# All rows of layer 1 turned by VectorE, and another order at the beginning, in a two-layer graph kernel on one Trainium2 core

## The chip, the core and the metric

The kernel runs on one core of one Trainium2 chip. The metric is the device time of one execution in microseconds; the median of several runs counts. TensorE multiplies, VectorE and ScalarE work elementwise, GpSimd takes small steps, and SyncE issues most of the transfers between memory and the on-chip buffer. [...]

## What is computed

4096 rows `x` of 512 numbers and a 4096 x 4096 matrix `adj` go through two layers. Layer 0 is softmax attention inside graphs of 128 rows each, so that one graph is one tile of 128 rows; layer 1 is attention over the nonzero entries of `adj` with 8 heads of 64 numbers.

```python
# layer 0
h = jnp.maximum(_layernorm(x), 0.0)
query, key, value = h @ Wq.T + bq, h @ Wk.T + bk, h @ Wv.T + bv
a = jnp.where(mask, query @ key.T * scale, 0.0)          # mask: same graph
scores = (a + adj + adj) * jnp.where(mask, 1.0, -1000000.0)
x = x + (softmax(scores) * mask) @ value
# layer 1
h = jnp.maximum(_layernorm(x), 0.0)
mx = jnp.einsum('nf,hfd->hnd', h, W)
logits = s_i[:, :, None] + t_j[:, None, :]               # s, t: mx times a_origin, a_dst
attn = softmax(where(adj > 0, logits, -inf))
x = x + concat over heads of attn @ mx
```

In layer 1 the term `s_i` cancels in the softmax. So each tile j of rows gives a `part`: exp(t_j) times its projected rows, and exp(t_j) itself. Then each of the 32 tiles of output is a product of the 0/1 mask of `adj` with all 32 parts, and a division.

## The kernel before

It runs in three stages. First `fold` turns the weights of query and key and multiplies them, so that one matrix M serves for both. Then layer 0 goes through 16 pairs of tiles; beside it, all of `adj` is read once, its mask packed into bytes and written to `a_d`, and the first tiles of layer 1 are projected. A second loop projects the other tiles of layer 1. The third stage is the aggregation, 32 times 96 matmuls.

A projection needs the rows of layer 1 turned (features on the partitions). There are two ways in the kernel: `relu_T` has TensorE turn the tile by four transposes; `turn` and `move` have VectorE turn it in 32x32 blocks, four tiles together, and bring the blocks to their places by a write to `hT_d` and a read of it. Before the change tiles 0 to 15 go the first way, 16 to 31 the second (`MIXED` = 16). NT is 32 tiles, KC 4 pieces of 128 features, BY 4, B 32, G 2.

```python
    def relu_T(ps_pool, hn, dst):

        pt = ps_pool.tile([P, KC, P], F32, name="pt")
        for k in range(KC):
            nc.tensor.transpose(pt[:, k, :], hn[:, ts(k, P)], ident)
        nc.scalar.activation(dst, pt, AF.Relu)
# ... (cut)
    def fold(sb, tmp, work, ps_t, ps_p, loads, first):
# ... (cut)
        wkT_sb = load_weight(tmp, wkT, "wkT_sb", KC, tag="lo")
        wqT_sb = load_weight(tmp, wqT, "wqT_sb", KC, tag="lo")
        loads()
# ... (cut)
        nat = []
        for n, wT in enumerate((wkT_sb, wqT_sb)):
            w = tmp.tile([P, KC, D], F32, name=f"w{n}", tag="lo")
            for k in range(KC):
                pt = ps_t.tile([P, KC, P], F32, name="pt")
                for m in range(KC):
                    nc.tensor.transpose(pt[:, m, :], wT[:, k, ts(m, P)], ident)
                nc.scalar.copy(w[:, :, ts(k, P)], pt)
                if n == 0 and k == 0:
                    rows = [spread_bias(b) for b in (bk_sb, bq_sb)]
            nat.append(w)
        wk, wq = nat
# ... (cut) u_col, c_sb: VectorE; then M = wq . wk on TensorE, u_col spread at m == 2
# ... (cut)
    def project1(ps_m, hT, w1x):

        pm = [ps_m.tile([P, D], F32, name="pp") for _ in range(2)]
        for g, n in ((1, HW + H), (0, HW)):
            for k in range(KC):
                nc.tensor.matmul(
                    pm[g][:, :n], hT[:, k, :], w1x[:, k, g * HW : g * HW + n],
                    start=(k == 0), stop=(k == KC - 1),
                )
        return pm
# ... (cut)
            def begin1():
                row = sb2.tile([P, D], F32, name="row1")
                nc.sync.dma_start(row, x1_d[len(rows1)])
                norm(row, row)
                rows1.append(row)

            def turned1(row):
                hT = sb2.tile([P, KC, P], F32, name="hT1")
                relu_T(ps_t, row, hT)
                return hT
# ... (cut)
            def prepare(i, hT, part):
                pm = project1(ps_p, hT, w1x)
                finish(weights(i, pm), pm, part)
# ... (cut)
                def attend(sT, v, g, t):
                    i = G * g + t
                    po = ps_p.tile([P, D], F32, name="pp")
                    nc.tensor.matmul(po, sT[:, t, :], v, start=True, stop=True)
                    x1 = sb.tile([P, D], F32, name="x1")
                    nc.vector.scalar_tensor_tensor(
                        x1, po, rs_all[:, i : i + 1], xg[g][:, t, :], ALU.mult, ALU.add
                    )
                    nc.scalar.dma_start(x1_d[i], x1)
# ... (cut)
                for g in range(NG):   # 16 pairs of tiles
# ... (cut) load_pair(g + 2); at g == 1: w1x = load_w1(pool1, sb)
                    s = scores(g, hT, gT, r, *look)
                    prepare_on(last)
                    if last:
                        begin1()
                    if not last:
                        ngT = queries(nhT)
                    sT = turned(s)
                    prepare_on(3 <= g and g % 2)

                    for _ in range({2: 1, NG - 2: 1, NG - 1: 0}.get(g, int(3 <= g and g % 2))):
                        begin1()
                    nvs = []
                    for t in range(G):
                        look_on(t)
                        if not last and t == 0:
                            nvs.append(values(nhT, t))
                        attend(sT, vs[t], g, t)
                        prepare_on(last and t == 0)
                        if not last and t:
                            nvs.append(values(nhT, t))
                    if not last:
                        hT, r, gT, vs, look = nhT, nr, ngT, nvs, nlook
                    if g + 2 < NG:
                        nhT, hns = turned0(g + 2)
                        nr = row_terms(hns)
# ... (cut) the second loop: VectorE, ScalarE, GpSimd and SyncE in written order
            def turn(i):
                c, b = divmod(i, BY)
                if b == 0:
                    blocks[c] = sb4.tile([P, P // B, KC, BY, B], F32, name="blocks")
                nc.vector.transpose(
                    blocks[c][:, :, :, b], rows[i].rearrange("p (k q f) -> p q k f", k=KC, f=B)
                )
                if b == BY - 1:
                    nc.sync.dma_start(hT_d[c], blocks[c].rearrange("p q k b r -> p q (k b r)"))

            def move(c):
                hT = sb5.tile([P, P // B, KC, P], F32, name="hT4")
                for q in range(P // B):
                    nc.sync.dma_start(
                        hT[ts(q, B)].rearrange("p u k m -> p u (k m)"),
                        hT_d[c, :, q].rearrange("(u f) w -> f u w", f=B),
                    )
                for u in range(BY):
                    hTs[c * BY + u] = hT[:, u]
# ... (cut)
                for i in range(n, NT):
                    far, near = i + AHEAD, i + 2
                    if near + 1 < MIXED:
                        load(near + 1)
                    load(far + 2)
                    if far % BY == 1 and MIXED + BY < far <= NT + 1:
                        move(far // BY - 1)
# ... (cut) from far == NT + 1 on: the mask of the first tile of the aggregation
                    low()
                    if far < NT:
                        of[far] = moments(rows[far])
                    if near < MIXED:
                        of[near] = moments(rows[near])
                    if MIXED < far <= NT:
                        turn(far - 1)
                    if i + 1 < MIXED:
                        hTs[i + 1] = sb2.tile([P, KC, P], F32, name="hT1")
                        relu_T(ps_t, rows[i + 1], hTs[i + 1])
                    pm = project1(ps_p, hTs[i], w1x)
                    if before:
                        low = finish(*before, later=True)
                    if near < MIXED:
                        norm(rows[near], rows[near], of[near])
                    if far < NT:
                        norm(rows[far], rows[far], of[far])
                    e = weights(i, pm)
                    halves = (1, 0)
                    if i < MIXED:
                        halves = (0,)
                        for h in range(H // 2, H):
                            nc.scalar.mul(
                                e[:, ts(h, HD)], pm[1][:, ts(h - H // 2, HD)],
                                e[:, ES + h : ES + h + 1],
                            )
                    before = (e, pm, part_tile(lo if i < LO else hi, i), halves)
                    if far < NT:
                        nc.scalar.activation(rows[far], rows[far], AF.Relu)
```

Pools hold the tiles: `bufs` is the number of buffers of one name, and a new tile waits until the oldest of its name has been read.

## Time and profile before

| what | value |
|---|---|
| device time, median of 3 | 938.12 us (937.1 to 938.38) |
| span of the profiled run | 936.6 us, 13145 instructions |
| beginning, up to the first `wv` product | 0 to 29.2 us |
| layer 0, 16 pairs | from there to about 355 us |
| second loop, projections of layer 1 | to about 443 us |
| aggregation | to the end |
| mean DMA rate over the span | 167 GB/s, 156.63 MB |
| `adj` loads | 64 of 1024 KB, median 12.2 us from issue to landing |

The page's groups give for each line of the kernel the engine, the operation, the tiles that it writes and reads, the shapes, the count, then busy time and mean duration of one. Matmuls are pipelined, so the distance between two starts and the duration of one differ. A wait is put down to what released it last. [...]

### The profile page before, as it was taken

What the parts mean: (1) busy time and instruction counts of PE and PEld (TensorE: products, weight loads), DVE (VectorE), ACT (ScalarE), POOL (GpSimd) and SP (SyncE); (2) the same over time, 40 slices, a digit from 0 to 9 for tenths busy, and PEclk for the clock granted to TensorE, in tenths of its full rate; (3) what the DMA queues carried; (4) which work ended last, traced back from release to release, by engine and by line L of the source; (5) the groups of instructions that cost most, each with busy time, mean ns of one, the idle gap of its engine ahead of it and who ended that gap; (6) DMA issues with size and microseconds to landing.
All of it is one profiled execution on the core that took longest, in us unless ns stands there. A gap on an engine that the chain in (4) does not pass through costs nothing.

```text
span 936.6 us, 13145 instructions
## 1 busy us (share of the span) xinstructions
PE 925.9 (99%) x4987; PEld 809.1 (86%) x4987; DVE 462.2 (49%) x992; ACT 268.1 (29%) x539; POOL 180.4 (19%) x344
## 2 busy tenths in 40 slices
PE   8999999999999999999999999999999999999997
PEld 5676677767677778888999999999999999999997
DVE  4678878777775447754463324242424233332412
ACT  4876576667672216532000000000000000000000
POOL 1311212331221116654101010110101010101010
PEclk9999999999999999999999999999999999999999
DMA  9999997989997114764123131312121222313111
GB/s 334 415 382 401 349 351 302 360 344 371 356 354 273 35 35 146 203 200 103 53 61 91 46 90 46 90 51 85 52 85 54 82 71 65 88 48 90 46 45 37
DMA packets 61062, 156.63 MB, mean 167 GB/s; under 512 B 6722, under 2 KB 23490, under 8 KB 52290
## 3 DMA queue, kind: packets, MB, share of 16 engines
q1 hardware_dynamic: 51058, 138.70, 42.9%
q10 hardware_dynamic: 9936, 17.05, 4.9%
q8 instruction: 40, 0.66, 0.3%
q14 instruction: 28, 0.23, 0.1%
HBM read 117.97 MB, written 37.75 MB: 166 GB/s over the span
## 4 chain that ended last, share of the span: by engine, by line
PE 94%; DMA 3%; ACT 2%; DVE 0%; SPq 0%; issue 0%; ACTq 0%
PE pg L315 51%; PE pp L264 12%; PE pp L461 11%; PE pp L473 11%; PE pp L546 3%; PE pss L519 3%; DMA a<-adj 2%; PE pt L136 2%; ACT junk L496 1%; PE pl L315 1%; DMA bv_sb<-bv 1%; PE pss L538 0%; ACT m_sb L239 0%; ACT gT L465 0%; DVE x L548 0%
## 5 line engine op out<-in xcount | busy, mean ns | idle before, releaser
L315 PE MATMUL pg<-part,ata 128*128 128x348 f32 (+1 forms) x1536 | 246.7, 321 | 0.0
L315 PEld LDWEIGHTS pg<-part,ata 128*128 128x128 f32 x1536 | 244.5, 188 | 0.1
L315 PE MATMUL pg<-part,atb 128*128 128x348 f32 x1472 | 236.4, 321 | 0.0
L315 PEld LDWEIGHTS pg<-part,atb 128*128 128x128 f32 x1472 | 234.2, 188 | 0.1
L329 ACT COPY tot<-pg 128x522 f32<-128x522 f32 x31 | 18.6, 600 | 453.4 <-PE pg L315 453.4
L496 ACT ACTIVATE junk<-a 128x2048 bf16<-128x2048 f32 (+15 forms) x92 | 124.5, 1353 | 36.3 <-DMA a<-adj 15.1
L264 PE MATMUL pp<-w1x,hT 128*128 128x256 f32 (+1 forms) x512 | 114.9, 383 | 0.5 <-DVE e L273 0.5
L473 PE MATMUL pp<-wv,hT 128*128 128x512 f32 x256 | 115.0, 593 | 0.3 <-ACT hT L137 0.3
L461 PE MATMUL pp<-hT,m_sb 128*128 128x256 f32 x512 | 113.2, 379 | 0.0
L301 DVE CAST atb<-at 128x4096 fp32r<-128x4096 fp8e4 x16 | 36.7, 2293 | 152.2 <-PE pg L315 152.2
L264 PEld LDWEIGHTS pp<-w1x,hT 128*128 128x128 f32 x512 | 96.0, 190 | 15.0 <-issue 0.9
L461 PEld LDWEIGHTS pp<-hT,m_sb 128*128 128x128 f32 x512 | 96.1, 190 | 12.9 <-issue 0.5
L301 DVE CAST ata<-at 128x4096 fp32r<-128x4096 fp8e4 (+1 forms) x17 | 36.8, 2167 | 140.4 <-PE pg L315 140.3
L146 DVE TENSOR_SCALAR a<-a 128x512 fp8e4<-128x512 f32 x256 | 96.8, 457 | 5.7 <-DMA a_d<-a 5.7
L473 PEld LDWEIGHTS pp<-wv,hT 128*128 128x128 f32 x256 | 47.8, 190 | 54.9 <-issue 53.1
L767 POOL COPY den_all<-tot 128x1 f32<-128x1 f32 x31 | 5.8, 186 | 365.0 <-DVE tot L330 365.0
L771 POOL TENSOR_TENSOR tot<-tot,row 128x512 f32<-128x512 f32 x31 | 39.9, 1288 | 62.2 <-DVE tot L335 58.1
L248 POOL TENSOR_TENSOR part<-e,part 128x522 fp32r<-128x522 f32 x32 | 41.1, 1285 | 12.9 <-ACT part L245 12.7
L122 POOL TENSOR_SCALAR ve<-mv 128x1 f32<-128x1 f32 x64 | 16.3, 259 | 131.1 <-DVE mv L120 131.0
L137 ACT ACTIVATE hT<-pt 128x512 f32<-128x512 f32 x48 | 26.9, 596 | 50.8 <-PE pt L136 40.5
L477 DVE TENSOR_TENSOR v<-pp,bv_sb 128x512 f32<-128x512 f32 x32 | 22.0, 687 | 39.2 <-PE pp L473 39.2
L292 DVE STREAM_TRANSPOSE at<-mw 128x1024 f32<-128x1024 f32 x32 | 39.6, 1238 | 2.1 <-DMA mw<-a_d 2.1
(113 smaller groups left out, 698.4 us busy)
## 6 DMA issues: line engine op xcount, KB each, us to landing
a<-adj SPq DMA_DIRECT2D x64, 1024.0 KB, 12.2
a_d<-a SPq DMA_DIRECT2D x32, 512.0 KB, 10.3
mw<-a_d SPq DMA_DIRECT2D x128, 128.0 KB, 3.9
row<-x_d SPq DMA_DIRECT2D x41, 256.0 KB, 3.5
xg<-x SPq DMA_DIRECT2D x16, 512.0 KB, 5.1
x_d<-x ACTq DMA_DIRECT2D x32, 256.0 KB, 4.3
out<-tot ACTq DMA_DIRECT2D x31, 256.0 KB, 3.7
rowm<-x_d SPq DMA_DIRECT2D x16, 256.0 KB, 5.2
```

Of the source, the lines that this page charges most:

```text
L146: nc.vector.tensor_scalar(a8v[:, u], av[:, u], 0.0, None, ALU.is_gt, saturate=False)
L248: nc.gpsimd.tensor_sub(dst[:, :, 1, :], e3, dst[:, :, 0, :].bitcast(F32))
L264: nc.tensor.matmul(pm[g][:, :n], hT[:, k, :], w1x[:, k, g * HW : g * HW + n], start=(k == 0), stop=(k == KC - 1),)
L292: nc.vector.transpose(at8.rearrange("p c n b -> p (c n b)").bitcast(F32).rearrange("p (c u n) -> p c u n", c=NW, n=B), mw.rearrange("p u ( ...
L301: nc.vector.tensor_copy(at[:, c0 * BY : c1 * BY].rearrange("p (c b) q -> p c b q", b=BY), at8[:, c0:c1].rearrange("p c q b -> p c b q"),)
L315: nc.tensor.matmul(pg[:, : 2 * CW1].rearrange("p (s w) -> p s w", s=2)[:, :, :n], at[:, j, :], part(j)[:, c, :, :n], start=(j == 0), stop= ...
L461: nc.tensor.matmul(pp[:, : G * P], m_sb[:, k, ts(m, P)], hT[:, k, :], start=(k == 0), stop=(k == KC - 1),)
L473: nc.tensor.matmul(pp, hT[:, k, ts(t, P)], wv[:, k, :], start=(k == 0), stop=(k == KC - 1))
L496: nc.scalar.activation(junk[:, c0:c1], a[:, c0:c1], AF.Exp, scale=2.0 * NEG, accum_out=sums[:, n : n + 1],)
L519: nc.tensor.matmul(pss[:, t, :], gT[:, k, ts(t, P)], hT[:, k, ts(t, P)], start=(k == 0), stop=(k == KC - 1),)
L546: nc.tensor.matmul(po, sT[:, t, :], v, start=True, stop=True)
L771: nc.gpsimd.tensor_add(num, num, row)
```

## The change

Tiles 0 to 15 of layer 1 lose their transposes on TensorE. They are normed, put through ReLU by ScalarE, turned by VectorE and moved through DRAM inside layer 0, one row tile in each pair of layer 0 from pair 1 on and two in the last (`fetch`, `begin`, `move`); eight are projected within layer 0 (`prepare`), at pairs 6, 8, 10, 12, 13 and three times in the last. The second loop has one way for all tiles, prepared `AHEAD` = 9 tiles before their use. Buffers make room for it: `gT`, `s` and `sT` have one instead of two, `diag` two instead of three, and `x1` is written over `xg`. TensorE's instructions of layer 0 stand in written order.

At the beginning, `bk` and `bq` are loaded by SyncE behind `wkT`, the broadcast of `bv` by SyncE behind `wvT`; ten transposes of the identity are put ahead of TensorE's work, and the products that spread the biases come after all of `wkT`'s transposes. The sums for `w1x` (`dots`) are spread over pairs 2 to 5. The byte order of the mask follows the new order of the tiles. Code that runs only for inputs outside the fast way is adapted; it isn't run here.

The diff, cut to its core:

```diff
-MIXED = NT // 2
-AHEAD = 8
+AHEAD = 9
+WARM = 10
# ... (cut)
-    nc.scalar.dma_start(bq_sb, bq)
     bk_sb = const.tile([P, KC], F32, name="bk_sb")
-    nc.scalar.dma_start(bk_sb, bk)
# ... (cut)
-        order = ("p (c b u q) -> p u c b q", "p (c u b q) -> p u c b q")[h]
-        av = a.rearrange(order, c=NW // 2, b=BY, q=B)
+        av = a.rearrange("p (c u b q) -> p u c b q", c=NW // 2, b=BY, q=B)
# ... (cut)
+        nc.sync.dma_start(bk_sb, bk)
+        nc.sync.dma_start(bq_sb, bq)
# ... (cut)
+        pt = ps_t.tile([P, KC, P], F32, name="pt")
+        for _ in range(WARM):
+            nc.tensor.transpose(pt[:, 0, :], ident, ident)
# ... (cut)
-                if n == 0 and k == 0:
+                if n == 0 and k == KC - 1:
# ... (cut)
-            rows1 = []
-
-            def begin1():
-                row = sb2.tile([P, D], F32, name="row1")
-                nc.sync.dma_start(row, x1_d[len(rows1)])
-                norm(row, row)
-                rows1.append(row)
-
-            def turned1(row):
-                hT = sb2.tile([P, KC, P], F32, name="hT1")
-                relu_T(ps_t, row, hT)
-                return hT
+            keep = prep.enter_context(
+                tc.tile_pool(name="keep", bufs=1, side="right", reuse_waits="tile")
+            )
+            blocks, hTs = {}, {}
+
+            def turn(i, row, pool):
+
+                c, b = divmod(i, BY)
+                if b == 0:
+                    blocks[c] = pool.tile([P, P // B, KC, BY, B], F32, name="blocks")
+                nc.vector.transpose(
+                    blocks[c][:, :, :, b], row.rearrange("p (k q f) -> p q k f", k=KC, f=B)
+                )
+                if b == BY - 1:
+                    nc.sync.dma_start(hT_d[c], blocks[c].rearrange("p q k b r -> p q (k b r)"))
+
+            def move(c):
+
+                hT = keep.tile([P, P // B, KC, P], F32, name="hT4", bufs=2)
+                for q in range(P // B):
+                    nc.sync.dma_start(
+                        hT[ts(q, B)].rearrange("p u k m -> p u (k m)"),
+                        hT_d[c, :, q].rearrange("(u f) w -> f u w", f=B),
+                    )
+                for u in range(BY):
+                    hTs[c * BY + u] = hT[:, u]
+
+            rows = {}
+
+            def fetch(i):
+                rows[i] = sb2.tile([P, D], F32, name="row1", bufs=1)
+                nc.sync.dma_start(rows[i], x1_d[i])
+
+            def begin(i):
+                norm(rows[i], rows[i])
+                nc.scalar.activation(rows[i], rows[i], AF.Relu)
+                turn(i, rows[i], keep)
+                if i + 1 < 2 * LO:
+                    fetch(i + 1)
# ... (cut)
-                    gT = sb.tile([P, KC, G * P], F32, name="gT")
+                    gT = sb.tile([P, KC, G * P], F32, name="gT", bufs=1)
-                        sb.tile([P, G, P], F32, name="diag", bufs=3),
+                        sb.tile([P, G, P], F32, name="diag"),
-                    s = sb.tile([P, G, P], F32, name="s")
+                    s = sb.tile([P, G, P], F32, name="s", bufs=1)
-                    sT = sb.tile([P, G, P], F32, name="sT")
+                    sT = sb.tile([P, G, P], F32, name="sT", bufs=1)
-                    x1 = sb.tile([P, D], F32, name="x1")
+                    x1 = xg[g][:, t, :]
                     nc.vector.scalar_tensor_tensor(
-                        x1, po, rs_all[:, i : i + 1], xg[g][:, t, :], ALU.mult, ALU.add
+                        x1, po, rs_all[:, i : i + 1], x1, ALU.mult, ALU.add
# ... (cut)
-                    nc.scalar.dma_start(bv_sb, bv.to_broadcast([P, D]))
+                    nc.sync.dma_start(bv_sb, bv.to_broadcast([P, D]))
# ... (cut)
+                with tc.manual_schedule(engines={mybir.EngineType.PE}):
+                    for g in range(NG):
+                        last = g + 1 == NG
+                        if g == 1:
+                            w1x, dots = load_w1(pool1, sb2, tag="e")
+                        if 2 <= g < 2 + KC:
+                            dots(g - 2)
+                        nlook = seen()
+
+                        def look_on(t):
+                            if not last:
+                                i = G * (g + 1) + t
+                                nlook[2].append(read(i, nlook[0][:, t, :], nlook[1][t]))
+
+                        s = scores(g, hT, gT, r, *look)
+                        if last:
+                            prepare()
+                        else:
+                            ngT = queries(nhT)
+                        sT = turned(s)
+                        if g in (6, 8, 10, 12, 13, NG - 1):
+                            prepare()
+
+                        if g == 1:
+                            fetch(0)
+                        for i in (NG - 2, NG - 1) if last else (g - 1,) if g > 1 else ():
+                            begin(i)
+                        if g > BY and g % BY == 1:
+                            move(g // BY - 1)
+                        if g + 2 < NG:
+                            load_pair(g + 2)
+                        nvs = []
+                        for t in range(G):
+                            look_on(t)
+                            if not last and t == 0:
+                                nvs.append(values(nhT, t))
+                            attend(sT, vs[t], g, t)
+                            if last and t == 0:
+                                prepare()
+                            if not last and t:
+                                nvs.append(values(nhT, t))
+                        if g == 1:
+                            begin(0)
# ... (cut)
+            upper = {j: part_tile(hi, j) for j in range(LO, NT)}
+                first = LO + AHEAD
+                for i in range(first - 1, first + 2):
+                    load(i)
+                move(LO // BY + 1)
+                norm(rows[first - 1], rows[first - 1])
+                nc.scalar.activation(rows[first - 1], rows[first - 1], AF.Relu)
                 before = None
+                for i in range(LO, NT):
+                    far = i + AHEAD
                     load(far + 2)
-                    if far % BY == 1 and MIXED + BY < far <= NT + 1:
+                    if far % BY == 1 and LO + AHEAD < far <= NT + 1:
# ... (cut)
-                    if near < MIXED:
-                        of[near] = moments(rows[near])
-                    if MIXED < far <= NT:
-                        turn(far - 1)
-                    if i + 1 < MIXED:
-                        hTs[i + 1] = sb2.tile([P, KC, P], F32, name="hT1")
-                        relu_T(ps_t, rows[i + 1], hTs[i + 1])
+                    if far <= NT:
+                        turn(far - 1, rows[far - 1], (keep, sb4)[(far - 1) // BY % 2])
# ... (cut)
-                    e = weights(i, pm)
-                    halves = (1, 0)
-                    if i < MIXED:
-                        halves = (0,)
-                        for h in range(H // 2, H):
-                            nc.scalar.mul(
-                                e[:, ts(h, HD)], pm[1][:, ts(h - H // 2, HD)],
-                                e[:, ES + h : ES + h + 1],
-                            )
-                    before = (e, pm, part_tile(lo if i < LO else hi, i), halves)
+                    before = (weights(i, pm), pm, upper[i])
```

## The prediction

> **What bounds the kernel now.** I read the page first, then the waits of TensorE before the aggregation, then TensorE's timeline at the seams, and last the waits of the DMA queue. The page:
>
> ```profile
> PE 925.9 (99%) x4987; PEld 809.1 (86%) x4987; DVE 462.2 (49%) x992; ACT 268.1 (29%) x539; POOL 180.4 (19%) x344
> PE 94%; DMA 3%; ACT 2%; DVE 0%; SPq 0%; issue 0%; ACTq 0%
> ```
>
> TensorE is busy 925.9 of 936.6 us and carries 94% of the chain that ended last. Busy does not mean at its peak, so I asked for TensorE's own waits in the first 445 us (columns: who waited for whom, us in total, times, longest):
>
> ```profile
> PE pt L198 <- DMA wkT_sb<-wkT: 3.9, 1, 3.9
> PE pp L264 <- DVE e L273: 0.5, 1, 0.5
> PE pp L236 <- ACT m_sb L239: 0.3, 1, 0.3
> PE pp L473 <- ACT hT L137: 0.3, 1, 0.3
> ```
>
> That is all: 3.9 us before the first weight arrives and 1.1 us later. One more 0.4 us hides behind pipelined ends: the chain between 197 and 212 us runs through an adjacency load, ScalarE's reads and `sT` (L540). So nothing that only shortens a wait of another engine can help. What helps is an instruction taken off TensorE, or TensorE's useful work beginning earlier. The timeline of TensorE shows the cost of what the change removes (columns: start us, us with pipelined end, line, operation, tiles, count):
>
> ```profile
> 358.95 0.60 PE L136 MATMUL pt<-ident,rown 128*128 128x128 f32 x4
> 359.39 3.67 PE L264 MATMUL pp<-w1x,hT 128*128 128x264 f32 x16
> 362.90 0.60 PE L136 MATMUL pt<-ident,rown 128*128 128x128 f32 x4
> 363.33 3.67 PE L264 MATMUL pp<-w1x,hT 128*128 128x264 f32 x16
> ```
>
> The starts count, not the durations: from the first transpose to the first matmul of the projection it is 359.39 - 358.95 = 0.44 us, from there to the next tile's transposes 3.51. So one tile's four transposes take some 0.435 us, 109 ns each, though each is listed with 272 ns, and a projection takes 3.51. Further on, ten projections without transposes go from 379.12 to 414.86 with one wait of 0.5: again 3.52 each.
>
> The beginning, again TensorE's timeline:
>
> ```profile
> 3.92 1.08 PE L198 MATMUL pt<-ident,wkT_sb 128*128 128x128 f32 x4 [3.92 <-DMA wkT_sb<-wkT]
> 4.80 1.91 PE L184 MATMUL pp<-ident,bk_sb 128*128 128x128 f32 x8
> 6.51 1.91 PE L184 MATMUL pp<-ident,bq_sb 128*128 128x128 f32 x8
> 8.21 2.00 PE L198 MATMUL pt<-ident,wkT_sb 128*128 128x128 f32 x12
> 10.12 2.63 PE L198 MATMUL pt<-ident,wqT_sb 128*128 128x128 f32 x16
> 12.59 0.59 PE L236 MATMUL pp<-w,w 128*128 128x512 f32 x1
> ```
>
> Sixteen bias matmuls take 3.41 us, 213 ns each; the sixteen transposes of `wqT` take 2.47 with small gaps. The array is slow at first, and the loads are slow too. The first piece of `wkT` lands 2.9 us after its issue and the others 7.1 after theirs, at about 9 us: with them goes the broadcast of `bv` on ScalarE's queue, which the chain shows from 1.74 for 6.89 us. The last of `wqT`, issued at 4.8 with some 7.2 to landing, is there at 12.0, and the product of the two weights starts at 12.59. Loads end this stage.
>
> [...]
>
> **The change, part by part.**
>
> 1. *Transposes off TensorE.* Before, tiles 0 to 15 of layer 1 are turned by TensorE: 36 matmuls from `row`, 28 from `rown`, together 64 x 109 ns = **7.0 us**, all on the path. ScalarE's 16 evacuations go too, off the path. In their place stand 16 passes of VectorE at 0.71 us and 16 of ReLU at 0.65 on ScalarE, both beside other work. That replacement costs no TensorE time.
>
> 2. *The beginning.* `bv` goes behind the weights on SyncE's queue, the biases behind `wkT`, and their sixteen matmuls behind all of `wkT`'s transposes. With nothing beside them, `wkT`'s other pieces should follow the first (3.8 us) at the pace that 256 KB have later, about 0.67 us at 390 GB/s: at 5.8 the last. `wqT` is issued some 0.9 us later than now, which leaves it behind `wkT` in the stream: 4 x 0.67 more and the small bias loads give about 8.7 to 9.3. Ten transposes of the identity need nothing but the identity (written from 1.24 for 0.29 us)[...]. The last transposes of `wqT` need 0.55 after the landing, so the weight product starts near 9.6 instead of 12.59: **3.0 us** (2 to 3.5). VectorE must have `u_col` by the third quarter of the product: four passes of 0.75 after `xg`'s statistics (landing 13.35 now, some 2 us earlier then), ready near 15, needed near 16.5. It just holds.
>
> 3. *Waits kept or removed.* Of the 0.3 + 0.3 + 0.4 + 0.5 us I take 0.5 as gone, because projections above tile 15 have the lighter VectorE step: below 16 it does two moments and two norms per tile (some 3.9 us with the turning, against a TensorE step of 3.94), afterwards one each, 0.68 + 0.18 + 0.55 + 0.71 + 2 x 0.40 = 2.9 us against 3.51.
>
> 4. *New work beside layer 0.* One pair of tiles moves 4 x 1024 KB of adjacency, 2 x 512 of mask bytes, 512 of `x` and 2 x 256 of `x1`: 6144 KB, 16.5 us at 380 GB/s, against TensorE's 18.4 us per pair. The change adds one row (256 KB) a pair, where before nine of the sixteen pairs had one, and every four pairs 1 MB out and 1 MB back (four blocks out, three back within the layer): 7 x 0.26 + 4 x 1.05 + 3 x 1.05 = 9.2 MB inside layer 0, 24 us of DMA. It has idle time at the end of the layer, but in the early pairs it has not:
>
> ```profile
> 61.00:80.00 19.00, 19.00 (x82) 12.96 (x81) 14.62 (x38) 10.71 (x21) 2.88 (x7) 1.00 0.98 393
> 80.00:98.00 18.00, 18.00 (x79) 12.52 (x77) 13.46 (x35) 11.84 (x23) 3.60 (x7) 1.00 1.00 377
> 298.00:320.00 22.00, 22.00 (x98) 15.90 (x97) 9.65 (x24) 4.98 (x14) 4.57 (x10) 1.00 0.29 106
> ```
>
> (columns: stretch, length, busy of TensorE, weight load, VectorE, ScalarE, GpSimd, clock, DMA share, GB/s). The mask bytes of a pair are issued about 14 us before its scores begin (the last at 85.18 for scores at 99.10). A pair with a 1 MB block move needs some 20 us of DMA, 1.5 to 2.5 more than TensorE without a projection; pairs 4 and 5, counted from 0, are such, so the lead falls to about 9 us. From pair 6 on a projection adds 3.5 us to TensorE in most pairs, and the lead returns. So the transfers stay hidden, narrowly. VectorE goes from some 14.5 to 15.8 of 18.4 us.
>
> 5. *Smaller buffers.* `gT`, `s`, `sT` fall to one buffer, `diag` to two. TensorE's order scores, queries, turn, values, attend lets each be read before the next is written. `x1` is now written over `xg`, so the next load of `xg` must wait for the store (4.3 us on the page) and not only for VectorE: it is issued near 200 instead of 196 in the pair that I looked at, lands about 5 later, and is turned at 217. About 7 us of slack remain of some 12.
>
> The aggregation from 443 us on has the same instructions. Sum: 7.0 + 3.0 + 0.5 = 10.5 us gained; for new short waits of TensorE (in-order queues of VectorE and ScalarE with less lead) I take off 1.5. **938.1 - 9.0 = 929.1 us**, 1.0% less.
>
> **Rivals.** *DMA becomes the bound of layer 0.* For it: the share of 0.98 to 1.00 above, and SyncE's queue, in which the wait for `xg`'s buffer already holds everything behind it:
>
> ```profile
> SPq L555 <- DVE x L548: 77.3, 9, 14.0
> SPq L402 <- PE pt L136: 45.9, 3, 32.3
> ```
>
> With the store in that wait, each pair could lose 4 to 5 us of issuing. Against it: adjacency loads are in flight ahead (11.4 us to landing), and a shrinking lead fills exactly this hole. If it comes true, 1 to 3 us of wait in 12 pairs give 935 to 955. *Scheduling:* TensorE now runs in written order while VectorE and ScalarE do not. If VectorE takes the statistics of a late `xg` ahead of `s`, `turned` waits, some 2 us a pair: 940 to 960. For it: now they already stand ahead of `s` at 200.7. *The beginning gains nothing:* if the loads arrive no earlier, or `u_col` is late, only part 1 remains: 931 to 932. *Everything hides,* waits included: 926.
>
> **Range and chances.** The favourable end is 7.0 + 3.5 + 1.0, 926.5; the unfavourable end inside the range is part 1 and half of part 2 with some 6 us of new waits. I take 925.5 to 936. The 2% line lies 18.8 us away; the change cannot gain that, since it removes 7 us of work and at most a few of waits. Slower by that needs either of the first two rivals in nearly every pair: 4%. Faster by 2%: 1%.
>
> **What would show it.** In the changed profile: no L136-type transposes of `row` or `rown`, 64 fewer; 3.51 us per projection from the end of layer 0 on; the weight product beginning near 9.6; pairs without projection still 18.4 us apart, those with one 21.9; the aggregation beginning near 433.5 instead of 442.8. Waits of TensorE for `hT` (late `xg`), `sT` or `v` of several us per pair would prove me wrong on parts 4 and 5, and a product that begins after 11.5 on part 2.

## The result, and the profile after

The changed kernel takes 960.43 us (median of 6 runs, 958.09 to 962.32), the kernel before 937.58 beside it (6 runs, 936.77 to 938.38): 1.0243 times as long, 95% interval 1.0227 to 1.0259. It was predicted to be 1.0% faster and is 2.4% slower.

The page after, the same two lines as before: busy time of the engines, and the chain that ended last.

```profile
PE 930.5 (97%) x4933; PEld 810.5 (84%) x4933; DVE 472.6 (49%) x1016; ACT 259.8 (27%) x507; POOL 176.1 (18%) x344
PE 84%; DVE 6%; DMA 4%; POOL 2%; issue 2%; ACT 1%; SPq 0%; ACTq 0%
```

TensorE has 54 instructions less (64 transposes removed, 10 of the identity added) and is busy 4.6 us **more**. Of the span of 960.5 us it is idle 30.0, before 10.7. So the 23.9 us of span are 19.3 of added waits and 4.6 of added busy time. By stretches (columns: stretch, length, busy time and number of instructions of TensorE, weight load, VectorE, ScalarE, GpSimd, clock, DMA share, GB/s), from the first scores to the last, and on to the aggregation:

```profile
44.00:367.00 323.00, 303.21 (x1244) 211.47 (x1243) 220.50 (x582) 181.43 (x353) 67.70 (x148) 0.97 0.84 308
367.00:465.50 98.50, 98.50 (x455) 84.53 (x454) 56.98 (x127) 30.16 (x74) 49.92 (x110) 1.00 0.58 165
```

In the kernel before the first of these stretches lasts 295.4 us with TensorE busy for 295.25. Now it lasts 27.6 longer, 19.8 of it idle, and TensorE is busy 8.0 longer, though six tiles' transposes (2.6 us) are gone from it: some 10 us of what remains runs slower. The granted clock of the stretch is 0.97 in place of 1.00. The DMA rate is 308 GB/s in place of 313, below the 377 and 393 that early pairs reached before the change. The second stretch is 4.9 us shorter than before: the ten tiles' transposes that it had, 4.4 us, and a wait of 0.5.

TensorE's waits in the first 470 us (who waited for whom, us in total, times, longest):

```profile
PE pt L134 <- DVE hn L128: 15.6, 8, 3.6
PE pp L495 <- ACT hT L135: 4.1, 5, 1.6
...
PE pp L242 <- ACT m_sb L245: 1.2, 1, 1.2
```

Before, there was no wait for `hn` at all. `hn` is the normalized `xg` of the next pair, which TensorE turns at a pair's end. One such place, TensorE's timeline (start us, us, line, operation, tiles, count, and in brackets the wait before it):

```profile
157.61 3.60 PE L507 MATMUL pp<-wv,hT 128*128 128x512 f32 x8
164.81 0.66 PE L134 MATMUL pt<-ident,hn 128*128 128x128 f32 x4 [3.61 <-DVE hn L128]
166.90 1.11 PE L134 MATMUL pt<-ident,hn 128*128 128x128 f32 x4 [1.43 <-DVE hn L128]
167.80 2.93 PE L553 MATMUL pss<-hT,gT 128*128 128x128 f32 x16
```

The wait is paid twice. First 3.61 and 1.43 us pass without work. Then the sixteen matmuls of the scores take 2.93 us; in the next pair, without such a wait, they take 1.95. Behind the waits at the ends of pairs 1, 5, 9 and 13 the trace has the clock at half (columns as for the stretches above), for 17.1 us in all:

```profile
84.50:87.90 3.40, 3.40 (x16) 3.22 (x15) 2.40 (x8) 1.49 (x5) 1.93 (x2) 0.50 0.46 133
166.40:169.90 3.50, 3.00 (x14) 3.00 (x15) 3.43 (x10) 1.12 (x2) 2.13 (x2) 0.51 0.90 253
255.20:262.00 6.80, 6.07 (x25) 5.69 (x26) 5.81 (x17) 3.17 (x9) 1.96 (x5) 0.50 0.65 236
347.40:350.80 3.40, 3.40 (x18) 3.24 (x17) 2.64 (x10) 1.80 (x3) 1.50 (x3) 0.51 0.02 5
```

VectorE's timeline shows why `hn` is late:

```profile
161.24 0.69 DVE L511 TENSOR_TENSOR v<-pp,bv_sb 128x512 f32<-128x512 f32 x1 [2.68 <-PE pp L507]
161.85 1.28 DVE L116 BATCH_NORM_STATS2 stats<-xg 128x6 f32<-128x512 f32 x2
...
163.12 0.66 DVE L116 BATCH_NORM_STATS2 stats<-row 128x6 f32<-128x512 f32 x1
164.21 0.55 DVE L128 TENSOR_SCALAR hn<-xg,mv,rstd 128x512 f32<-128x512 f32 x1 [0.42 <-POOL rstd L122]
```

VectorE sits idle for 2.68 us in front of the second `v`, which needs TensorE's value product. The statistics stand behind `v` in its queue, so they begin only when TensorE has nothing left to do. The fixed order of VectorE's instructions has moved with the change. In the kernel before, the statistics of the next `xg` stand ahead of `v` and of the additions of `x1` in every pair, here in pair 5:

```profile
142.16 0.67 DVE L118 BATCH_NORM_STATS2 stats<-xg 128x6 f32<-128x512 f32 x1
...
152.87 0.68 DVE L477 TENSOR_TENSOR v<-pp,bv_sb 128x512 f32<-128x512 f32 x1
```

In the changed one they stand behind them, or between them, in the pairs 1, 4, 5, 9 and 13 (counted from 0), and these are exactly the pairs at whose end TensorE waits for `hn`. From one pair's scores to the next TensorE's own work is 18.4 us without and 21.9 with a projection; the pairs 5, 9 and 13 take 5.9, 6.6 and 4.2 us more, the five pairs 20.7, all pairs together 29.5.

The loads of `xg` are not what is late here. In these five pairs `xg` had landed 8.9, 0.8, 3.3, 8.7 and 8.7 us before its statistics began. VectorE's own waits for `xg` from 44 to 370 us are even shorter than in the kernel before (first line):

```profile
DVE stats L118 <- DMA xg<-x: 9.0, 5, 3.7
DVE stats L116 <- DMA xg<-x: 2.5, 1, 2.5
```

SyncE's queue has new waits too (first 370 us):

```profile
SPq L435 <- DVE blocks L414: 66.6, 9, 14.4
SPq L589 <- DMA x_d<-xg: 27.6, 7, 6.8
SPq L109 <- DMA x_d<-xg: 21.6, 2, 11.3
```

L435 fetches a row for layer 1 into the one `row1` buffer, and waits for VectorE to turn the row before. L589 loads `xg` and waits for the store of `x1` out of the same buffer. The third is odd: an adjacency load waits for a store of `x1`, with which it shares nothing. SyncE's timeline around that stop (start us, us, line, transfer, count):

```profile
153.16 0.35 SPq L536 DMA_DIRECT2D a_d<-a  x1
154.47 11.02 SPq L109 DMA_DIRECT2D a<-adj  x2
166.07 0.34 SPq L536 DMA_DIRECT2D a_d<-a  x1
```

The two adjacency loads of the second line are 10.7 us apart (154.47 and 165.16). In the trace each of the 425 transfers of SyncE and ScalarE carries one of eight semaphores, 100 to 107, shared between them and taken in turn, 53 or 54 transfers on each. The load at 165.16 carries number 103, as did the `x1` store that ScalarE issued at 157.73. The store landed at 165.08; the load followed 0.07 us later. That is no single case: on the numbers 100 to 106, whose landings the trace has in full, none of the 365 transfers that follow another of their number was issued before that one had landed, whatever it moved. Between the first and the last pair's scores the kernel before issues 138 transfers, the changed one 159.

After layer 0 nothing was lost. TensorE, in one line:

```profile
381.31 84.56 PE L270 MATMUL pp<-w1x,hT 128*128 128x264 f32 x384
```

These are 24 projections of 16 matmuls from 381.31 to 465.52, 3.51 us each and without any gap. The aggregation begins at 465.5 instead of 442.8, and takes 495.0 us, before 493.8.

And the beginning:

```profile
11.07 7.03 PE L242 MATMUL pp<-w,w 128*128 128x512 f32 x16
...
20.36 3.70 PE L242 MATMUL pp<-w,w 128*128 128x512 f32 x8 [1.24 <-ACT m_sb L245]
...
29.28 3.27 PE L507 MATMUL pp<-wv,hT 128*128 128x512 f32 x7 [0.91 <-ACT hT L135]
```

The weight product begins 1.5 us earlier than before and the `wv` product at 29.28 against 29.2: the gain is waited away for ScalarE, whose copy of `m_sb` stands behind a read of an adjacency tile that begins at 17.92 us (before 18.49). Scores of pair 0 start at 44.03 us, before at 43.98; those of the last pair at 367.07, before at 339.45. The whole loss lies between these two.

### The profile page after: what moved, and what is told of

Read it like the earlier page. It is cut to its first block, busy times and chain, and to the rows that moved or that the text cites. A ratio compares the mean times of both kernels' runs of the same rounds, so it can differ in the third digit from the quotient of the medians. Undisturbed runs are those within 1.5% of the kernel's fastest.

```text
span 960.5 us, 13021 instructions
## 1 busy us (share of the span) xinstructions
PE 930.5 (97%) x4933; PEld 810.5 (84%) x4933; DVE 472.6 (49%) x1016; ACT 259.8 (27%) x507; POOL 176.1 (18%) x344
## 4 chain that ended last, share of the span: by engine, by line
PE 84%; DVE 6%; DMA 4%; POOL 2%; issue 2%; ACT 1%; SPq 0%; ACTq 0%
PE pg L321 50%; PE pp L270 11%; PE pp L495 10%; PE pp L507 6%; PE pss L553 2%; DMA a<-adj 2%; PE pp L580 1%; POOL rstd L122 1%; DVE hn L128 1%; DMA x_d<-xg 1%; PE pl L321 1%; DVE stats L116 1%; PE pt L134 1%; DVE xg L582 1%; POOL ve L120 1%
## 5 line engine op out<-in xcount | busy, mean ns | idle before, releaser
L495 PE MATMUL pp<-hT,m_sb 128*128 128x256 f32 x512 | 115.2, 384 | 4.2 <-ACT hT L135 4.1
L270 PEld LDWEIGHTS pp<-w1x,hT 128*128 128x128 f32 x512 | 96.6, 190 | 15.8 <-issue 1.3
L279 DVE TENSOR_TENSOR e<-pp,e 128x256 f32<-128x256 f32 x64 | 25.1, 410 | 52.4 <-ACT e L447 39.8
L254 POOL TENSOR_TENSOR part<-e,part 128x522 fp32r<-128x522 f32 x32 | 40.7, 1272 | 14.5 <-ACT part L251 14.5
L120 POOL TENSOR_SCALAR ve<-mv 128x1 f32<-128x1 f32 x64 | 18.5, 295 | 128.5 <-DVE mv L118 128.5
L122 POOL TENSOR_TENSOR rstd<-ve,neghalf 128x1 f32<-128x1 f32 x64 | 38.0, 599 | 3.7
```

The costliest lines, as they stand in the source:

```text
L120: nc.gpsimd.tensor_scalar(ve, mv[:, 1:2], EPS, None, ALU.add)
L122: nc.gpsimd.tensor_tensor(rstd, ve, neghalf, ALU.pow)
L254: nc.gpsimd.tensor_sub(dst[:, :, 1, :], e3, dst[:, :, 0, :].bitcast(F32))
L270: nc.tensor.matmul(pm[g][:, :n], hT[:, k, :], w1x[:, k, g * HW : g * HW + n], start=(k == 0), stop=(k == KC - 1),)
L495: nc.tensor.matmul(pp[:, : G * P], m_sb[:, k, ts(m, P)], hT[:, k, :], start=(k == 0), stop=(k == KC - 1),)
```

## The experiments

**Theory.** Loads of layer 0 come too late, because the change has more of them in a queue that stands more often, and because `x1` now lies in `xg`'s buffer. **First rival:** the loads do not matter; VectorE's new fixed order holds TensorE. **Second rival:** the added bytes alone saturate the transfers. All times are medians beside the kernel before on the same chip, in brackets the ratio to it with its 95% interval; that kernel took 937.5 to 939.0 us each time.

### Changes to the changed kernel

`room` makes place for a fourth `xg` buffer and is the control; `xg4` has it.

```diff
-v = sb.tile([P, D], F32, name="v", bufs=4)
+v = sb.tile([P, D], F32, name="v", bufs=3)      # room, xg4
-junk = sb.tile([P, NH], BF16, name="junk", bufs=1)
+junk = sb.tile([P, NH], FP8, name="junk", bufs=1)
-xg[g] = sb.tile([P, G, D], F32, name="xg", bufs=3)
+xg[g] = sb.tile([P, G, D], F32, name="xg", bufs=4)   # xg4 only
```

> The changed kernel with v in three buffers instead of four and ScalarE's unread output junk in one byte instead of two; this only makes room for the next kernel and is its control. Every theory: like the changed kernel, about 960 us (within 3).

> The control with four buffers for xg instead of three. Theory A (the load of xg waits for the store of x1 out of the same buffer, so hn comes late and TensorE waits[...]): with a fourth buffer the load waits for a store that is a whole pair older; most of the 15.6 us of waits for hn and of the slow clock after them go, and the time falls to 932 to 940 us. Rival B (layer 0 is bound by the transfers that the change adds): nothing gained, 955 us or more. Rival D (smaller buffers and TensorE's written order): nothing gained either.

Measured: `room` 960.7 us (1.0238, 1.0217 to 1.0259), `xg4` 959.8 (1.0239, 1.021 to 1.0268). The fourth buffer brings nothing. VectorE's order stayed that of the change, and TensorE still waits 14.7 us for `hn`. This speaks for the first rival: as long as that order stands, earlier room for `xg` does not count.

`notrip` leaves out the write of the blocks to DRAM and their reading back for the first four groups of four tiles; the projections take the blocks as they lie, so the features of 16 tiles are in another order and the output is not the reference's.

```diff
-if b == BY - 1:
+if b == BY - 1 and c >= 4:
     nc.sync.dma_start(hT_d[c], ...)
 def move(c):
+    if c < 4: hTs[c * BY + u] = blocks[c][:, u] ...; return
```

> The changed kernel without the write to and the read from DRAM of the first four blocks (16 tiles); the projections read the blocks as VectorE left them, so these tiles' features are in a wrong order. Leaves out 4 MB written and 4 MB read, all but 1 MB of it inside layer 0. Rival B (transfers bind): falls to 935 to 942 us. Theory A: the store of x1 still stands between, small gain of 2 to 8 us by shorter queues, 952 to 958 us.

Measured: 965.5 us (1.0288, 1.0264 to 1.0312), slower than with the trip. It does not clear the trip of blame: VectorE's fixed order came out differently again, TensorE's waits for `hn` fell to 2.7 us and those for `hT` rose to 12.8. Taken by itself the run is inconclusive, but it showed that the order has to be held fixed before transfers can be compared.

`row2` gives the fetched row two buffers on top of `room`. VectorE's order is that of the change from pair 4 on.

```diff
-rows[i] = sb2.tile([P, D], F32, name="row1", bufs=1)
+rows[i] = sb2.tile([P, D], F32, name="row1", bufs=2)
```

> The changed kernel with two buffers for the fetched row (and the smaller v and junk that made room, alone 960.7 us without any gain). VectorE's written order is that of the change from pair 4 on; only SyncE's queue no longer stands at the row's fetch until VectorE has turned the row before (66.6 us of such waits in the change). If VectorE's fixed order is what holds the tiles in the change, nothing moves: 958 to 962 us, with 14 to 16 us of TensorE waits on hn. If the standing of SyncE's queue at the fetch is what makes x late, then some 5 to 10 us come back, 950 to 956, and the waits on hn fall below 8.

Measured: 958.15 us (1.0223, 1.0206 to 1.024). The waits of SyncE for `blocks` at the fetch are gone, and TensorE's first wait is unchanged:

```profile
PE pt L134 <- DVE hn L128: 15.1, 8, 3.6
```

With `xg4` and the landing times above this settles what holds TensorE in the changed kernel as it is: VectorE's order, and neither the buffer of `xg` nor the standing at the row's fetch. What a better order is worth it does not say.

### The order written by hand

`ord4` is `xg4` with VectorE's instructions in written order: the statistics of the next `xg` ahead of `v` and the additions in every pair, and the load of the pair after next issued at the pair's top. `ord3` is the same with three `xg` buffers (and the change's `v` and `junk`). `ord4nt` is `ord4` without the blocks' trip through DRAM (as in `notrip`, features of 16 tiles in another order).

```diff
-with tc.manual_schedule(engines={mybir.EngineType.PE}):
+with tc.manual_schedule(engines={mybir.EngineType.PE, mybir.EngineType.DVE}):
# ... (cut) at the top of a pair:
+    if g + 2 < NG: load_pair(g + 2)
# ... (cut) after the sums of the scores, ahead of v and x1:
+    ofs = [moments(xg[g + 2][:, t, :]) for t in range(G)]
+    hns = normed(g + 2, ofs)
+    nr = row_terms(hns)
```

> The changed kernel with xg in four buffers, its load at the top of the pair, and VectorE's instructions of layer 0 in written order: the statistics of the next xg stand after the first eight mask steps, ahead of v and of the two additions of x1, in every pair; same arithmetic, same transfers. Theory E (in some pairs VectorE's queue has the statistics of xg behind v and both additions, so that hn cannot come before TensorE is through with the pair): the waits for hn and the slow clock behind them go, 927 to 936 us. Rival B (transfers bind): 950 us or more, with waits for adjacency loads moved elsewhere.

> The same written order of VectorE, with three buffers for xg as in the changed kernel, so that the load still waits for the store of x1 out of the same buffer. Theory E alone: as good as with four buffers, within 3 us. Theory A together with E (both the order and the reuse cost): VectorE now waits in front of the statistics with v and the additions behind it, 8 to 20 us more than with four buffers.

> The version with written order and four buffers, without the write to and the read from DRAM of the first four blocks (features of these tiles in a wrong order). Theory E: the transfers are hidden, within 2 us of the same version with them. Rival B: 5 us or more faster.

Measured: `ord4` 956.49 us (1.021, 1.0183 to 1.0236), `ord3` 961.3 (1.0242, 1.022 to 1.0264), `ord4nt` 940.71 (1.0032, 1.0012 to 1.0053). The first rival predicts that the order alone brings the loss back. By the medians it brings nothing with three buffers and some 4 us with four, although the waits for `hn` are down to 1.8 us in `ord3` and gone in `ord4`. The stretch from the first pair's scores to the last pair's, in the profiled executions, shows more. It takes 295.5 us in the kernel before. The changed one takes 27.6 more, `xg4` 25.2, `ord3` 17.1, `ord4` 9.1 and `ord4nt` 1.6. So in layer 0 the written order (with the earlier load) is worth some 10 us, a fourth buffer 8 on top of it (2 without it), and the blocks' trip 7 on top of both. These are single executions: that of `ord4` is its fastest, 951.94 us of 951.94 to 960.05. Behind the last scores `ord3` and `ord4` give 10.0 and 9.2 us back. There TensorE now waits in the second loop, where the changed kernel has no gap:

```profile
PE pp L270 <- DVE e L279: 7.5, 2, 5.8
```

VectorE stands ahead of it, 3.94 us for the write of the blocks and 4.34 for a row. What limits `ord4` within layer 0, VectorE and TensorE in pair 6 show:

```profile
173.33 0.69 DVE L116 BATCH_NORM_STATS2 stats<-xg 128x6 f32<-128x512 f32 x1 [7.05 <-DMA xg<-x]
```

```profile
178.51 2.08 PE L597 MATMUL pp<-v,sT 128*128 128x512 f32 x2 [4.52 <-DVE e L279]
180.38 4.97 PE L521 MATMUL pp<-wv,hT 128*128 128x512 f32 x8
```

Now VectorE waits 7.05 us for a late `xg`, with everything else behind it, and pair 6 takes 30.3 us. TensorE waits 4.52 and then needs 4.97 us for eight matmuls that take 3.60 elsewhere. So the load is the next limit, close behind the first: VectorE's waits for `xg`, 2.5 us in the changed kernel, come to 54.8 in `ord3`, 21.7 in `ord4` and 12.0 in `ord4nt`. Three `xg` buffers cost about 5 us more than four once the order is fixed. And without the blocks' trip 16 us come back by the medians: `ord4` and `ord4nt` ran beside each other, and the trip is all that they differ in besides the place where the blocks lie. Of the 12.5 us between their profiled spans 7.4 lie in layer 0 and 6.2 behind it (`ord4nt` begins 1.2 later). Whether the trip costs by its bytes, by the number of its transfers or by SyncE's waiting for the blocks, these runs do not separate.

`best1` was meant to beat the kernel before: `ord4` with SyncE's queue in written order as well, the row's fetch last in each pair.

```diff
+engines={mybir.EngineType.PE, mybir.EngineType.DVE, mybir.EngineType.SP}
+if g > 1 and not last: fetch(i + 1)     # after everything else of the pair
```

> Transposes off TensorE as in the changed kernel, four buffers for xg, and VectorE's and SyncE's queues of layer 0 in written order: SyncE takes the load of xg and the reads of the blocks first in a pair and the row for the next pair last; the block of tiles 16 to 19 goes to the other buffer and the read of tiles 12 to 15 comes one tile later, so that the second loop doesn't wait for the end of layer 0. Same arithmetic, same transfers as the changed kernel. Theory F (the loss is the order in which two fixed queues, SyncE's and VectorE's, take late things ahead of urgent ones, with DMA close to full): 928 to 938 us. Rival B (the transfers are simply too many): 945 us or more whatever the order.

Measured: 967.4 us (1.0304, 1.0286 to 1.0322), a miss. VectorE now waited 56.0 us for the row and 11.6 for `xg`. Putting the row last in SyncE's queue only chose what came late.

### Parts of the change put on the kernel before

`start` has the change's beginning alone (order of loads, ten transposes of the identity, bias matmuls behind `wkT`). `small` has its smaller buffers for `gT`, `s`, `sT` and `diag`. `alias` only writes `x1` over `xg`:

```diff
-x1 = sb.tile([P, D], F32, name="x1")
+x1 = xg[g][:, t, :]
```

> The kernel before with the beginning of the change alone: bk and bq on SyncE's queue behind wkT, the bv broadcast behind wvT, ten transposes of the identity first, the bias products behind wkT's transposes. As predicted: 2 to 3.5 us faster, 934.5 to 936. Rival, from the changed trace (the product starts at 11.07 but ScalarE's queue, in which the evacuation of m_sb stands behind reads of adjacency, holds TensorE to the same 29.28): within 1 us of before.

> The kernel before, with only the buffer counts of the change that are not part of x1: gT, s and sT with one buffer, diag with two. The prediction's part 5 held these harmless, because TensorE reads each before the next is written: 937 to 939 us, the ratio 1.00 within 0.2%. The rival: with one buffer ScalarE and VectorE must wait for TensorE's reads before they write the next gT, s, sT, and queue behind that; then some 0.3 us in each of 16 pairs, 942 to 945, and TensorE shows waits on sT or gT.

> The kernel before with one part of the change alone: x1 is written over xg instead of into a tile of its own. Theory A: TensorE gets waits for hn as in the changed kernel, 945 to 958 us. Rival B: within 2 us of before, since the load then only comes some 5 us later where 12 us of slack were seen.

Measured: `start` 937.89 us (1.0008, 0.9985 to 1.003), `small` 936.36 (0.9984, 0.9965 to 1.0002), `alias` 952.42 (1.0155, 1.0132 to 1.0177). The beginning brings nothing, the smaller buffers cost nothing, and the two-line edit of `alias` costs some 14 us (13.5 by the medians, 14.5 by the ratio). Its SyncE queue:

```profile
SPq L555 <- DMA x_d<-xg: 161.9, 17, 14.3
```

In each pair the load of the next `xg` waits for the store, and the adjacency loads behind it wait along. So VectorE gets `xg` late: its waits, 9.0 us in five pairs before, grow to

```profile
DVE stats L118 <- DMA xg<-x: 31.4, 9, 5.4
```

### Added transfers on the kernel before

The next four leave everything as it is and add transfers that nobody needs: the stored `x1` of tiles 0 to 27 is copied to another place in DRAM. `traf` copies 28 times 256 KB, 7.3 MB read and written, from ScalarE's queue; `traf2` twice that; `tiny` 28 times 8 KB; `trafp` 28 times 256 KB from GpSimd's queue.

```diff
+if i >= 4:
+    nc.scalar.dma_start(tr_d[u, i], x1_d[i - 4])                     # traf, traf2
+    nc.scalar.dma_start(tr_d[i][0:16, 0:128], x1_d[i - 4][0:16, 0:128])  # tiny
+    nc.gpsimd.dma_start(tr_d[i], x1_d[i - 4])                        # trafp
```

> The kernel before with 28 copies of 256 KB from DRAM to DRAM added on ScalarE's queue, two a pair from pair 2 on: 7.3 MB, as much as the changed kernel writes and reads for its blocks inside layer 0; nothing reads them. Rival B: 8 us or more slower than before. Theory F: DMA has room for it, up to 3 us slower.

> The same with twice the copies, 14.7 MB. Rival B: 20 us or more slower than before. Theory F: here the reserve of the 16 pairs is about used up, 3 to 15 us slower.

> The kernel before with the same 28 added transfers on ScalarE's queue as in the run with 7.3 MB, of the same form but 8 KB each instead of 256. [...] Theory G (the added transfers cost by their number: each takes a turn, and holds up its queue and the later loads of adjacency): most of the 16.5 us remain, 945 to 956 us. Rival B (they cost by their bytes): within 3 us of before.

> The kernel before with the 28 copies of 256 KB issued by GpSimd, whose transfers don't take turns with those of SyncE and ScalarE; VectorE's order is that of before, word for word. Theory G: the bytes alone cost little, up to 4 us. Rival B: 10 us or more.

Measured: `traf` 954.38 us (1.0166, 1.0149 to 1.0184), `traf2` 962.76 (1.0272, 1.025 to 1.0295), `tiny` 951.74 (1.0149, 1.013 to 1.0168), `trafp` 943.52 (1.0054, 1.0022 to 1.0086). The second rival expected the bytes to be the cost. But 28 copies of 8 KB, 0.2 MB, cost 14.2 us of the 16.5 that 28 copies of 256 KB cost. SyncE's queue of `tiny`:

```profile
SPq L112 <- DMA tr_d<-x_d: 17.3, 7, 5.4
SPq L112 <- DMA x_d<-x: 15.1, 6, 6.3
```

L112 is the adjacency load. It waits for copies that it does not need, and for stores of `x1`, 15.1 us where this stop came to 10.9 in the kernel before: the turn of eight, with more numbers used up. But little of this comes through: VectorE waits 11.8 us for `xg` (9.0 before), ScalarE 17.0 for the adjacency (15.1 before). The cost lies in ScalarE's own queue. In the built order a copy does not stand two pairs behind the store of the row that it copies, as it is written, but close behind it: the first is issued at 61.62 us, when two stores have been issued. So ScalarE stands until the store has landed, and with it `hT`, which ScalarE writes for TensorE. Pair 4, ScalarE and then TensorE:

```profile
114.46 1.51 ACTq L552 DMA_DIRECT2D x_d<-x  x2
122.24 0.52 ACTq L554 DMA_DIRECT2D tr_d<-x_d  x1
122.86 1.48 ACT L497 ACTIVATE junk<-a 128x1536 bf16<-128x1536 f32 x1 [8.70 <-DMA x_d<-x]
...
124.34 0.58 ACT L138 ACTIVATE hT<-pt 128x512 f32<-128x512 f32 x1
```

```profile
125.46 9.28 PE L462 MATMUL pp<-hT,m_sb 128*128 128x256 f32 x32 [5.08 <-ACT hT L138]
```

The store landed at 122.22 and the copy followed at 122.24. In the kernel before, without a copy, the same `hT` is written from 117.67 on. TensorE waits for `hT` behind such a copy at the pairs 1, 4, 12 and 13, and these take 13.3 us more than before, of 14.2 for all pairs; in `traf` the same four take 14.8 of 16.0. GpSimd's copies carry eight other semaphores, 111 to 118, in the trace of `trafp`. They wait for the same stores, but no `hT` stands behind them, and there the same bytes cost 5 to 6 us. So these runs show what a transfer costs in the queue of an engine that has other work behind it. They do not show that the number of transfers in the turn of eight costs time, and the changed kernel, whose added transfers stand in SyncE's queue, does not have this cost.

From the cheap copies of `trafp` it was tempting to move the change's new transfers to GpSimd. `gp` does that with the changed kernel's row fetches, block writes and block reads in layer 0, `gpo4` with those of `ord4`.

```diff
-nc.sync.dma_start(rows[i], x1_d[i])        # likewise hT_d[c] and hT
+nc.gpsimd.dma_start(rows[i], x1_d[i])
```

> The changed kernel with the row loads, the block writes and the block reads of layer 0 issued by GpSimd instead of SyncE; nothing else is edited, but VectorE's order comes out otherwise, with the statistics of xg ahead of v in all but one pair. Theory G with the order of VectorE as its means: most of the loss goes, 926 to 942 us. Rival B: 952 us or more.

> The version with VectorE's written order and four buffers for xg (956.5 us), with the same transfers issued by GpSimd. Theory G: near the version without the blocks' way through DRAM (940.7), 932 to 944 us. Rival B: 952 us or more.

Measured: `gp` 982.7 us (1.0467, 1.0445 to 1.0489), `gpo4` 964.04 (1.0288, 1.0263 to 1.0313): two misses in the wrong direction, 22 and 8 us slower than with SyncE. In `gp` the wait of the `xg` load for the `x1` store grew from 27.6 us to

```profile
SPq L590 <- DMA x_d<-xg: 191.8, 17, 17.3
```

The row's fetch no longer held the load of `xg` back, so the load came to the head of the queue earlier and stood there for its buffer, adjacency loads behind it. VectorE then waits 51.5 us for `xg`, 2.5 in the changed kernel, which fits the loss. It is not shown to be all of it: VectorE's order moved as well, and the profiled execution is the slowest of five, 990.09 us. For `gpo4`, which has four buffers, no single cause was found.

### The two costs together

`aliastraf` is the kernel before with `alias` and `traf` together. It still has all transposes on TensorE.

> The kernel before with the two costs that were measured one by one put together: x1 written over xg (alone 952.4) and 28 copies of 256 KB from DRAM to DRAM on ScalarE's queue (alone 954.4). It still has the 64 transposes on TensorE. Theory that late loads, from these two causes, are what the change lost: the costs overlap in part, since both make the same queue stand: 957 to 967, that is as much as the change plus the 7 us of its removed transposes (967). Rival that VectorE's order in the change is the main cause: then the two together bring little more than each alone, 952 to 957, and the rest of the change's loss needs the order. A full sum would be 968 to 970.

Measured: 969.02 us (1.0328, 1.0299 to 1.0357), 31.4 us more than before; alone the two had cost 13.5 and 16.5 by their medians. By the ratios it is 3.28% against 1.55% + 1.66% = 3.21%: they add up in full. The changed kernel, with its 7 us of removed transposes put back, would stand at 967.4, close by. In `aliastraf` the statistics of the next `xg` stand ahead of `v` and of the additions in every pair, as in the kernel before, and yet TensorE waits:

```profile
PE pp L462 <- ACT hT L138: 22.7, 9, 6.7
```

```profile
126.05 8.62 PE L462 MATMUL pp<-hT,m_sb 128*128 128x256 f32 x32 [5.74 <-ACT hT L138]
309.00 9.30 PE L462 MATMUL pp<-hT,m_sb 128*128 128x256 f32 x32 [6.66 <-ACT hT L138]
```

The page counts 933.0 us of busy TensorE against 925.9, with the same work: 7.1 us of slower matmuls. With 22.7 of waits for `hT` and 1.8 for a `part` that makes 31.6, the whole loss. The 32 query matmuls take 8.62, 8.86 and 9.30 us after waits of 5.74, 2.41 and 6.66, but 7.17 after the other six (0.63 to 2.92) and 7.07 without a wait.

Taken by its time alone this looks like the change's loss, made from late loads. The trace says otherwise. VectorE waits 15.7 us for `xg`, half of what it waits in `alias`, and at all nine waits for `hT` ScalarE stands at a copy until a store of `x1` has landed, with `hT` behind it, as in `tiny`. The changed kernel has no such copies, so the nearness of 969.02 to 967.4 proves nothing about it.

What holds layer 0 of the changed kernel is therefore read from the runs above: first VectorE's order, behind it the late `xg` of a shared buffer, behind that the blocks' trip. Each repair uncovered the next wait. No version beat the kernel before.

## Why the prediction was wrong

1. **Transposes off TensorE: right.** 7.0 us of work left the path, and the second loop runs at 3.51 us a projection without a gap, as predicted.

2. **The beginning, +3.0 us: wrong, the rival "the beginning gains nothing" came true.** The product began at 11.07 instead of the predicted 9.6, and the step that failed is the next one: I followed the loads and `u_col`, and not ScalarE. Its copy of `m_sb` came late, behind a read of the adjacency (1.24 us of wait at 20.36), then `hT` (0.91), and by the `wv` product all was gone. What the ten transposes of the identity were to bring was my estimate; measured, the eight matmuls for `bk` behind them begin 125 ns apart (6.62 to 7.62 us) instead of 213. `start` alone: ratio 1.0008.

3. **Waits after tile 15 gone: right.** The second loop has none of them.

4. **VectorE "goes from some 14.5 to 15.8 of 18.4 us": the step that failed in the changed kernel.** It counted VectorE's busy time and took the order of its queue as given. Busy time was no bound, 220.5 us of the stretch's 323. But in five pairs the statistics of `xg` came to stand behind `v` or the additions; TensorE waited 15.6 us for `hn`, and these pairs took 20.7 of the 29.5 us. **"So the transfers stay hidden, narrowly"** held for the loads of `xg` only because VectorE was later still (2.5 us of waits). With the order repaired they are not hidden: 54.8 us of waits in `ord3`, 21.7 in `ord4`, and without the blocks' trip layer 0 is 7.4 us shorter. The step compared 9.2 MB with a rate of 380 GB/s and with a lead of about 9 us, and left out that new transfers wait for VectorE at the head of SyncE's queue, 66.6 us at the row's fetch.

5. **"About 7 us of slack remain" for `xg`: wrong; the rest of the step right.** One pair was read, and its 12 us were counted up to TensorE's turning. VectorE, which comes first and has other work queued behind the statistics, had no slack: in the kernel before it waits for `xg` in five pairs, 9.0 us, and in that very pair 1.4. With `x1` over `xg` this grows to 31.4, and `alias` loses some 14 us by this edit alone. The store it waits for lands 6.0 us after its issue in the changed kernel, not 4.3, and the load carries the whole queue behind it. The smaller buffers are harmless: `small`, 0.9984.

**The rivals.** "Scheduling", 940 to 960, named the very wait of the changed trace: the statistics in the wrong place of VectorE's queue; they stand behind `v` and not, as I had feared, ahead of `s`. "DMA becomes the bound", 935 to 955, named the next limit behind it. I gave both together 4%, holding them unlikely to come true in nearly every pair. They did not need to: three pairs lost 16.7 us, the other twelve 12.8.

**The term of the sum that was far too small:** "for new short waits" of TensorE, from VectorE's and ScalarE's queues, I took off 1.5 us. 19.3 us of waits came, and some 10 more of slower matmuls, for which the sum had no term. The trace shows them behind waits: the sixteen matmuls of the scores take 2.93 us instead of 1.95 after waits of 3.61 and 1.43, and at the end of pair 13 a single wait of 2.47 us is followed by 3.4 us at half clock. In `aliastraf` the 32 query matmuls take 8.86 us after a wait of 2.41 and 7.17 after one of 2.92, so the length of the wait alone does not decide.

**What stays open.** The costs do not simply add up, since each repair uncovers another wait: the steps of 10, 8 and 7 us for order, buffer and trip hold in that sequence, for layer 0, from one profiled execution each. Why VectorE's order changed was not traced to one line of the change. A version of the changed kernel with `x1` in a buffer of its own was not run.

## What to carry to other kernels

Before you take work off the bounding engine by sending it round through DRAM, ask of each new transfer not only how many bytes it has but in whose queue it stands, what it waits for there, and what stands behind it. Look in the trace for loads that wait for stores with which they share nothing, and for an engine with work of its own that stands at the issue of a transfer. Treat the written-down order of a side engine as part of the change, compare it between the two kernels, and hold it fixed before you compare anything else. Read slack at the first engine that uses the data, not at the last. TensorE's waits in layer 0, 19.8 us, cost half as much again here in slower matmuls, some 10 us, so the idle time in this profile understates them.

## What was not expected of the hardware

- After some waits of a few microseconds, not after all, TensorE is slow for the next few microseconds: eight value matmuls 4.97 instead of 3.60 us after 4.52 us of wait, 32 query matmuls 9.30 instead of 7.07 after 6.66. In layer 0 of the changed kernel this came to some 10 us beside 19.8 us of waits, with 17.1 us at half clock; one wait of 2.47 us was enough for 3.4 of them.
- Twenty-eight transfers of 8 KB cost this kernel 14.2 us, nearly as much as 28 of 256 KB with 16.5: ScalarE, which issued them, stood until a store had landed, and TensorE's input stood behind it.
- The same 28 copies of 256 KB cost 5 to 6 us when GpSimd issued them; but taking needed transfers from SyncE to GpSimd made the changed kernel 22 us slower.
